# Second part of a two-level Winograd kernel in a written order, its buffers over those of the first part, bias through ScalarE

## The chip, the cores and the metric

The kernel runs on one core of one Trainium2 chip. The metric is the device time of one execution in microseconds. The engines named below are TensorE (PE; its weight loads are a row of their own, PEld), VectorE (DVE), ScalarE (ACT), GpSimd (POOL) and SyncE (SP), which here only issues transfers. Each engine works through its own queue in order and waits on semaphores for the others.

## The reference

Everything is fp32. There are 8 batches of 256 tokens with 1024 features, and 8 adapter matrices of 1024 x 1024, one of which is chosen for each batch by an index.

```python
w = weight[adapter_ids]                       # (8, 1024, 1024)
y = einsum('bsi,boi->bso', x, w)
base_out = einsum('btd,od->bto', y, base_W) + base_b
logits = einsum('btd,nd->btn', y, router_W) + router_b      # 15 columns
topk_p, topk_i = top_k(softmax(logits), 8)
w = einsum('btk,btke->bte', topk_p, onehot(expert_map[topk_i]))
h = einsum('btd,erd->bter', y, A)             # 8 experts of rank 16
lora = einsum('bter,eor->bto', h * w[..., None], B) * 2.0
out = x + base_out + lora
```

## The kernel before, in words

**First part (lines 161 to 431).** For each batch b it computes y = W x with one level of Winograd's scheme: seven block products instead of eight, each of 16 matmuls (128x128 by 128x128), accumulated in three PSUM tiles pa, pb, pc. VectorE makes the sums of weight blocks (`first_sum`, `other_sums`) and of x blocks (`turns`), and adds PSUM results into y. The weight tiles `wt` (8 buffers of 8 KB a partition) come by transfers. Two further things are threaded through this loop, each one batch behind. `project` multiplies y of batch b-1 by the router's and the LoRA's down matrices, ScalarE copies h and takes Exp; `weigh` (VectorE) makes softmax, the eight largest, and hw = h times its weights; `turn` transposes hw on TensorE and ScalarE copies it to `hwTs`. `prepare(n)` makes, on VectorE, a share of the 14 sums and raw blocks of base_W that the second part's left sides need, and stores them to two DRAM tiles, left_raw and left_sum (n = 0 to 3 writes entries 0 to 2, n = 4 to 7 entries 3 to 6). This whole part stands under `manual_schedule` for TensorE, VectorE, ScalarE and SP: their instructions run in the order in which the program writes them. After the loop come the turn of batch 6, the projection of batch 7, and `weigh` and `turn` of batch 7 (lines 428 to 431).

**Second part (lines 435 to 607).** base_W y is done with two levels of the same scheme, for two groups of four batches. A group has seven outer products, called with left numbers 0, 1, 3, 5, 4, 6, 2; each (`product`, line 470) has again seven inner blocks of 4 matmuls (128x128 by 128x256), in the order a11, s1, s2, a12, s3, s4, a22. Four of the seven carry LoRA terms: 8 more matmuls by hwT and up (line 461), two each in blocks s1, a12, s4 and a22. A product loads its two left tiles, makes four differences t1 to t4 of its right side on VectorE (line 487, tiles `lt`), and drains PSUM seven times: four times with `take` (a copy by ScalarE, line 504, where there is no base to add; an add by VectorE, lines 497 and 500, where there is) and three times with `add`. Blocks a11, s2, s3 and a22 accumulate one after the other in the same PSUM tile pa, so each of the last three may begin only when the drain of the one before has read pa. In the last product of all, pa is split in two tiles, pa and pe.

The right sides are y's blocks and running differences of them: b11, t2, b12 and b21 are remade on VectorE with whole-block subtractions of 2048 elements a partition (lines 584, 586, 593, 598). Four of the products give results; `residual` loads the tile xt of x and adds it and the bias (line 557, two scalar_tensor_tensors of 128x256), and `store` writes the result out.

The second part is not under `manual_schedule`. The framework's planner orders its instructions, and it may mix them with the end of the first part. Buffers are placed pool by pool: when the pools of the first part close, those of the second take their place in memory from the start, and a tile may be written only when all tiles that lay there before have been read for the last time. Here the first pool of the second part is t2, then the `lt` tiles, then u and v, the result tiles q and the tiles xt.

Of the kernel before, what the change touches and what calls it, by code (L numbers as in the profile page):

```python
# [27 lines left out]
def kernel(  # L28
# [21 lines left out]
    KH = 4  # L50
# [12 lines left out]
    wpool = ctx.enter_context(tc.tile_pool(name="w", bufs=8))  # L63
    dram = ctx.enter_context(
# [11 lines left out]
    em_i = const.tile([P, N], I32, name="em_i")  # L76
    bb = const.tile([P, KC], F32, name="bb")

# [37 lines left out]
    def weigh(h, ex, route, rpool):  # L116
# [28 lines left out]
        hw = rpool.tile([P, NTT, ER], F32, name="hw")  # L145
# [7 lines left out]
    def turn(b, hw, ident, ps_t):  # L153

        pt = ps_t.tile([P, S], F32, name="pt")
        for j in range(NTT):
            nc.tensor.transpose(pt[:, ts(j, P)], hw[:, j, :], ident)  # L157
        nc.scalar.copy(hwTs[b // GB][:, b % GB // 2, b % 2, :], pt)


    with ExitStack() as phase:
        cpool = phase.enter_context(tc.tile_pool(name="c1", bufs=1))
        xpool = phase.enter_context(tc.tile_pool(name="x", bufs=2))
        tpool = phase.enter_context(tc.tile_pool(name="t", bufs=2))
        rpool = phase.enter_context(tc.tile_pool(name="route", bufs=2))
        mpool = phase.enter_context(tc.tile_pool(name="m", bufs=1))
# [7 lines left out]
        ps_t = phase.enter_context(  # L174
            tc.tile_pool(name="ps_t", bufs=1, space=bass.MemoryType.PSUM)
        )

        ident = cpool.tile([P, P], F32, name="ident")
        make_identity(nc, ident)
# [5 lines left out]
        def constants():  # L185
            nc.sync.dma_start(rb, router_b.to_broadcast([P, N]))
            nc.sync.dma_start(em_i, emap.to_broadcast([P, N]))
            nc.sync.dma_start(bb, base_b)
            nc.sync.dma_start(ar_sb.rearrange("p k n -> p (k n)"), ar)
            nc.vector.tensor_copy(em_f, em_i)  # L190
            for e in range(E):
                nc.vector.tensor_scalar(
                    route[:, e, :], em_f, float(e), SCALING, ALU.is_equal, ALU.mult
                )
# [113 lines left out]
        def turns(x):  # L308

            b11, b12, b21, b22 = x[:, 0, 0], x[:, 0, 1], x[:, 1, 0], x[:, 1, 1]  # L310
            t1 = tpool.tile([P, KH, P], F32, name="t1")
            nc.vector.tensor_sub(t1, b12, b11)
            t2 = tpool.tile([P, KH, P], F32, name="t2")
            nc.vector.tensor_sub(t2, b22, t1)
            t4 = tpool.tile([P, KH, P], F32, name="t4")
            nc.vector.tensor_sub(t4, b21, t2)
            nc.vector.tensor_sub(b12, b22, b12)
            return t1, t2, t4
# [21 lines left out]
        EN = mybir.EngineType  # L340
# [13 lines left out]
        for b in range(B):  # L354
# [22 lines left out]
            if waiting:  # L377
                turn(*waiting, ident, ps_t)
# [28 lines left out]
            else:  # L407
                block(pa, q["a21"], b12, False)
                nc.vector.tensor_add(out(1, 1), pa, m5)
                hw = weigh(h, ex, route, rpool)  # L410
                waiting = b - 1, hw
                block(pc, q["s4"], b22, False)
                if last:
                    nc.vector.tensor_add(out(0, 1), pc, u2)
                    prepare(b)
                block(pa, q["a22"], t4, False)
                nc.scalar.copy(out(1, 0), pa)
# [10 lines left out]
        turn(*waiting, ident, ps_t)  # L428

        h, ex = project(B - 1, ar_sb, rpool, ps_h, (1, 0))  # L430
        turn(B - 1, weigh(h, ex, route, rpool), ident, ps_t)
# [3 lines left out]
    with ExitStack() as phase:  # L435
        tpool = phase.enter_context(tc.tile_pool(name="t2", bufs=1))
        lpool = phase.enter_context(tc.tile_pool(name="l2", bufs=8))
        mpool = phase.enter_context(tc.tile_pool(name="m2", bufs=1))
        qpool = phase.enter_context(tc.tile_pool(name="q2", bufs=6))
        xpool = phase.enter_context(tc.tile_pool(name="x2", bufs=3))  # L440
# [5 lines left out]
        )  # L446

# [22 lines left out]
        def product(left, right, base, into, u=None, hw=None, split=False):  # L470


            ra = wpool.tile([P, NS, 4 * P], F32, name="wt")
            nc.sync.dma_start(
                ra.rearrange("p s f -> p (s f)"), left_raw[left].rearrange("p s f -> p (s f)")
            )
            su = wpool.tile([P, NS, 3 * P], F32, name="wt")
            nc.sync.dma_start(
                su.rearrange("p s f -> p (s f)"), left_sum[left].rearrange("p s f -> p (s f)")
            )  # L480
            a11, a12, s3, a22 = (ra[:, :, ts(n, P)] for n in range(4))
            s1, s2, s4 = (su[:, :, ts(n, P)] for n in range(3))
            b11, b12, b21, b22 = right[:, 0, 0], right[:, 0, 1], right[:, 1, 0], right[:, 1, 1]

            def minus(x, y):
                t = lpool.tile([P, 2, S], F32, name="lt")
                nc.vector.tensor_sub(t, x, y)  # L487
                return t

            t1 = minus(b12, b11)  # L490
            t2 = minus(b22, t1)
            t3 = minus(b22, b12)
            t4 = minus(b21, t2)

            def add(dst, acc, other):
                if acc[0] is acc[1]:
                    nc.vector.tensor_add(dst, acc[0], other)  # L497
                else:
                    for mi in range(2):
                        nc.vector.tensor_add(dst[:, mi], acc[mi][:, mi], other[:, mi])  # L500

            def take(dst, acc, i, j):
                if base is None:
                    nc.scalar.copy(dst, acc[0])
                else:
                    add(dst, acc, base(i, j))
# [7 lines left out]

            pa = 2 * [ps.tile([P, 2, S], F32, name="pa")]
# [5 lines left out]
            c11, c12, c21, c22 = into(0, 0), into(0, 1), into(1, 0), into(1, 1)  # L521
            block(pa, a11, b11, True)
            take(c11, pa, 0, 0)
            block(pc, s1, t1, True, *term(1, 1))
            take(c22, pc, 1, 1)
            block(pa, s2, t2, False)
            take(c12, pa, 0, 1)
            block(pb, a12, b21, True, *term(0, 0))
            add(c11, pb, c11)
            yield 0, 0, c11  # L530
            block(pa, s3, t3, False)
            add(c22, pa, c22)
            yield 1, 1, c22
            block(pc, s4, b22, False, *term(0, 1))
            add(c12, pc, c12)
            yield 0, 1, c12
            block(pa, a22, t4, False, *term(1, 0))
            take(c21, pa, 1, 0)
            yield 1, 0, c21
# [3 lines left out]

        for g in range(B // GB):
            y, hw = ys[g], hwTs[g]

# [3 lines left out]
            def residual(oh, th, i, j, q):  # L550

                n = number(oh, th, i, j)
                xt = xpool.tile([P, 2, S], F32, name="xt")
                nc.sync.dma_start(xt.rearrange("p m t -> p (m t)"), xr[n])
                for mi in range(2):
                    c = oh * KH + 2 * i + mi
                    nc.vector.scalar_tensor_tensor(  # L557
                        q[:, mi], xt[:, mi], bb[:, c : c + 1], q[:, mi], ALU.add, ALU.add
                    )

            def store(oh, th, i, j, q):
                n = number(oh, th, i, j)
                nc.sync.dma_start(outq[n], q.rearrange("p m t -> p (m t)"))

            def finish(*r):
                residual(*r)
                store(*r)

            def flat(t):
                return t.rearrange("p i j k o -> p (i j k o)")  # L570

            b11, b12, b21, b22 = y[:, 0, 0], y[:, 0, 1], y[:, 1, 0], y[:, 1, 1]
            u = mpool.tile([P, 2, 2, 2, S], F32, name="u")
            v = mpool.tile([P, 2, 2, 2, S], F32, name="v")
# [3 lines left out]


            for _ in product(0, b11, None, at(u)):  # L580
                pass
            for r in product(1, b21, at(u), fresh, 0, hw[:, 0]):
                finish(0, 0, *r)
            nc.vector.tensor_sub(flat(b11), flat(b12), flat(b11))
            t2 = tpool.tile([P, 2, 2, 2, S], F32, name="t2")
            nc.vector.tensor_sub(flat(t2), flat(b22), flat(b11))
            for _ in product(3, t2, at(u), at(u)):
                pass
            for _ in product(5, b11, at(u), at(v), 1, hw[:, 1]):
                pass  # L590
            for r in product(4, b22, at(v), fresh, 2, hw[:, 1]):
                finish(0, 1, *r)
            nc.vector.tensor_sub(flat(b12), flat(b22), flat(b12))
            for i, j, q in product(6, b12, None, fresh):
                nc.vector.tensor_add(u[:, i, j], u[:, i, j], q)
                nc.vector.tensor_add(q, v[:, i, j], q)
                finish(1, 1, i, j, q)
            nc.vector.tensor_sub(flat(b21), flat(b21), flat(t2))
            end = g == B // GB - 1
            if end:  # L600
                residual(1, 0, 1, 0, u[:, 1, 0])
            for i, j, q in product(2, b21, at(u), fresh, 1, hw[:, 0], end):
                if end and (i, j) == (1, 0):
                    for mi in range(2):
                        nc.sync.dma_start(outq[number(1, 0, 1, 0), :, ts(mi, S)], q[:, mi])
                else:
                    finish(1, 0, i, j, q)
# [69 lines left out]
```

## Time and profile before

| | |
|---|---|
| median of 3 runs | 445.47 us (445.07 to 446.3) |
| profiled execution | 445.35 us |
| its span | 443.6 us |
| granted TensorE clock | 0.999 |
| TensorE busy | 436.4 us (98%) |
| VectorE busy | 306.4 us (69%) |
| ScalarE busy | 36.3 us (8%) |
| first block of the second part starts | 241.51 us |
| last matmul record starts | 439.71 us or just after (two records, 0.59 us together) |

The span runs from the first to the last instruction of the profiled execution; the device time has 1.77 us around it. An fp32 matmul leaves two records on TensorE and two on the row of its weight loads. In a timeline a line has the start, the length (of all merged instructions), the engine, the program's line, the operation, the tiles, the count, and in square brackets the idle time before it and who ended it. Matmul records overlap by about 0.16 us, so the distance from start to start says more than a length.

### The profile page before, as it was taken

The page shows a single profiled execution, that of the slowest core. Times are in us where ns is not written, and L with a number is a line of the kernel's source. Part 1 is how long each engine was busy: PE and PEld are TensorE (multiplying, and loading weights), DVE is VectorE, ACT ScalarE, POOL GpSimd, SP SyncE. Part 2 cuts the span into 40 slices and gives each one's busy share as a digit, 9 for nine tenths or more (in the row PEclk, how much of TensorE's full clock was granted, in tenths as well). Part 3 has the DMA queues.
Part 4 walks back from the last instruction along what each step waited for, and adds up shares of the span by engine and source line. Part 5 has one row for each costly group of instructions (what it writes and reads, how often), then busy time and mean ns, then how long its engine had stood idle before and what let it go on. Part 6 is the DMA issues. An engine that isn't in the chain of part 4 may idle for free.

```text
span 443.6 us, 7251 instructions
## 1 busy us (share of the span) xinstructions
PE 436.4 (98%) x2996; PEld 410.2 (92%) x2996; DVE 306.4 (69%) x523; ACT 36.3 (8%) x73; POOL 0.7 (0%) x6
## 2 busy tenths in 40 slices
PE   6999999999999999999999999999999999999997
PEld 6999999999999999999999788888888888888885
DVE  0579597582973967949629599746598399546494
ACT  1110101011011110110111100000100100000100
POOL 0000000000000000000000000000000000000000
PEclk9999999999999999999999999999999999999999
DMA  7998978678597687894872968622969738601463
GB/s 235 399 396 305 327 268 310 225 284 291 190 287 258 250 273 277 287 329 140 271 295 103 389 243 280 242 97 100 310 228 276 277 112 287 236 0 53 139 183 125
DMA packets 35122, 106.19 MB, mean 239 GB/s; under 512 B 3090, under 2 KB 6930, under 8 KB 31890
## 3 DMA queue, kind: packets, MB, share of 16 engines
q1 hardware_dynamic: 35090, 105.74, 68.7%
q8 instruction: 23, 0.38, 0.3%
q14 instruction: 9, 0.07, 0.1%
HBM read 84.49 MB, written 21.23 MB: 238 GB/s over the span
## 4 chain that ended last, share of the span: by engine, by line
PE 93%; DVE 4%; DMA 1%; SPq 1%; issue 0%
PE pa L214 24%; PE pa L452 21%; PE pc L214 12%; PE pc L452 11%; PE pb L214 7%; PE ph L97 6%; PE pb L452 5%; PE pc L461 3%; PE pb L461 2%; PE pa L461 1%; DMA wt<-in_w_dram 1%; DVE lt L487 1%; PE pe L452 1%; PE pt L157 0%; DVE w L144 0%
## 5 line engine op out<-in xcount | busy, mean ns | idle before, releaser
L452 PE MATMUL pa<-lt,wt 128*128 128x256 f32 x324 | 78.4, 380 | 0.0
L452 PEld LDWEIGHTS pa<-lt,wt 128*128 128x128 f32 x324 | 61.1, 190 | 9.5 <-DVE u L497 0.6
L214 PE MATMUL pa<-x,wt 128*128 128x128 f32 x512 | 59.9, 275 | 2.1 <-DMA wt<-in_w_dram 2.1
L214 PEld LDWEIGHTS pa<-x,wt 128*128 128x128 f32 x512 | 58.5, 192 | 2.5 <-issue 1.3
L214 PE MATMUL pa<-t,wt 128*128 128x128 f32 x480 | 56.1, 275 | 0.0
L214 PEld LDWEIGHTS pa<-t,wt 128*128 128x128 f32 x480 | 54.8, 192 | 0.0
L106 DVE TENSOR_TENSOR lg<-ph,rb 128x30 f32<-128x30 f32 x8 | 1.5, 189 | 47.3 <-ACT h L105 47.3
L97 PE MATMUL ph<-ar_sb,y 128*128 128x143 f32 x256 | 32.7, 285 | 0.0
L97 PEld LDWEIGHTS ph<-ar_sb,y 128*128 128x128 f32 x256 | 31.9, 190 | 0.0
L214 PE MATMUL pb<-x,wt 128*128 128x128 f32 x256 | 30.0, 275 | 0.0
L214 PE MATMUL pc<-t,wt 128*128 128x128 f32 x256 | 29.9, 275 | 0.0
L214 PE MATMUL pc<-x,wt 128*128 128x128 f32 x256 | 29.9, 275 | 0.0
L214 PEld LDWEIGHTS pb<-x,wt 128*128 128x128 f32 x256 | 29.2, 192 | 0.0
L214 PEld LDWEIGHTS pc<-t,wt 128*128 128x128 f32 x256 | 29.2, 192 | 0.0
L214 PEld LDWEIGHTS pc<-x,wt 128*128 128x128 f32 x256 | 29.2, 192 | 0.0
L452 PE MATMUL pc<-lt,wt 128*128 128x256 f32 x112 | 27.9, 379 | 0.0
L557 DVE SCALAR_TENSOR_TENSOR q<-xt,bb,q 128x256 f32<-128x256 f32 x62 | 27.0, 478 | 0.4
L452 PE MATMUL pc<-y,wt 128*128 128x256 f32 x96 | 24.1, 379 | 0.0
L452 PE MATMUL pb<-y,wt 128*128 128x256 f32 x96 | 24.1, 379 | 0.0
L452 PEld LDWEIGHTS pc<-lt,wt 128*128 128x128 f32 x112 | 21.3, 190 | 2.9
L325 DVE TENSOR_TENSOR wt<-wt 128x2048 f32<-128x2048 f32 (+1 forms) x9 | 18.5, 2051 | 6.5 <-DMA wt<-in_wq_dram 6.5
L452 PE MATMUL pa<-y,wt 128*128 128x256 f32 x92 | 22.1, 379 | 0.0
(117 smaller groups left out, 482.7 us busy)
## 6 DMA issues: line engine op xcount, KB each, us to landing
wt<-in_wq_dram SPq DMA_DIRECT2D x21, 1024.0 KB, 6.3
wt<-left_raw SPq DMA_DIRECT2D x14, 1024.0 KB, 5.7
wt<-left_sum SPq DMA_DIRECT2D x14, 768.0 KB, 6.5
xt<-in_xr_dram SPq DMA_DIRECT2D x32, 256.0 KB, 3.4
out_dram<-q SPq DMA_DIRECT2D x31, 256.0 KB, 2.5
x<-in_xq_dram SPq DMA_DIRECT2D x7, 1024.0 KB, 6.3
wt<-in_w_dram SPq DMA_DIRECT2D x7, 1024.0 KB, 5.4
spare<-in_bq_dram SPq DMA_DIRECT2D x4, 1024.0 KB, 5.5
```

Of the source, the lines that this page charges most:

```text
L97: nc.tensor.matmul(ph[:, j], lhsT=y[:, k // KH, th, k % KH // 2, bi, k % 2, ts(j, P)], rhs=ar_sb[:, k, :], start=(j == order[0] and k == 0 ...
L106: nc.vector.tensor_add(lg, ph[:, :, ER:], rb.unsqueeze(1).to_broadcast([P, NTT, N]))
L214: mm = nc.tensor.matmul(acc[:, m // 2, m % 2, :], lhsT=left[:, k, ts(m, P)], rhs=right[:, k, :], start=(first and n == 0), stop=(k == KH - 1),
L325: nc.vector.tensor_add(q["s1"][:, h], q["a21"][:, h], q["a22"][:, h])
L452: nc.tensor.matmul(acc[mi][:, mi, :], lhsT=left[:, 2 * k + mi, :], rhs=right[:, k, :], start=(first and k == 0 and (mi == 0 or acc[0] is n ...
L461: nc.tensor.matmul(acc[mi][:, mi, :], lhsT=up[:, ts(mi, P)], rhs=hw, start=False, stop=True, skip_group_check=True,)
L487: nc.vector.tensor_sub(t, x, y)
L557: nc.vector.scalar_tensor_tensor(q[:, mi], xt[:, mi], bb[:, c : c + 1], q[:, mi], ALU.add, ALU.add)
```

## The change

The second part is put under `manual_schedule` too, and its order is written out.

- Each of the seven products has seven gaps, one ahead of each block. In a gap the program first appends steps to two queues, `soon` and `later`, and then runs up to two of them (`fill(2)`), `soon` first. The steps are VectorE instructions: the differences of the next product (two in gap 0, one each in gaps 3 and 4), the subtractions that remake b11, t2, b12 and b21, now in quarters of 512 elements a partition, the joint additions of product 5, and the residual additions with the stores behind them. The drains of the blocks stand in the program between the gaps.
- The left tiles are loaded by `load_left`: those of products 0 and 1 near the end of the first part, those of product n + 2 in gap 5 of product n. The tiles of x are loaded in gaps 0 to 3 of the product that needs them (6 buffers instead of 3).
- The four differences of the first product are made in the last turn of the first loop, ahead of `prepare(7)`. In the first part and the second the difference tiles share one pool, `tt`, of 6 buffers.
- The turn of batch 7 moves from the end of the first part to behind the first product of the second. Its hw lies in a pool of its own; the identity and the transposes' PSUM tile now live through both parts.
- The pools are opened in another order: in the first part x, m, c1, then the routing pool and prep; in the second m2 (u and t2), q2, x2, v. So u and t2 lie over x, q over m and c1, the tiles of x over the routing pool and prep.
- The bias is added by ScalarE: in products 0 and 5 of a group each `take` becomes two activations (Identity, 128x256) with the bias as a pointer operand. Product 5 uses the difference of the two halves of the bias, made once by a VectorE subtraction in `constants`. The residual is then one VectorE add of 128x512.

The matmuls are the same in number and form. The diff, cut to its core:

```diff
@@ weigh, load_left, differences
-    def weigh(h, ex, route, rpool):
+    def weigh(h, ex, route, rpool, hwpool):
...
-        hw = rpool.tile([P, NTT, ER], F32, name="hw")
+        hw = hwpool.tile([P, NTT, ER], F32, name="hw")
...
+    def differences(right):
...
+                t[n] = tpool.tile([P, 2 * S], F32, name="tt").rearrange(
+                    "p (k o) -> p k o", k=2
+                )
+                x, y = (t[v] if isinstance(v, int) else v for v in (of, less))
+                nc.vector.tensor_sub(t[n], x, y)
...
+        return [minus(1, b12, b11), minus(2, b22, 1), minus(3, b22, b12), minus(4, b21, 2)]
...
@@ constants
+            nc.vector.tensor_sub(bb[:, KH:], bb[:, KH:], bb[:, :KH])
...
@@ last turn of the first loop, and its end
                 if last:
                     nc.vector.tensor_add(out(0, 1), pc, u2)
+                    left[0] = load_left(lefts[0])
+                    terms = [step() for step in differences(ys[0][:, 0, 0])]
                     prepare(b)
                 block(pa, q["a22"], t4, False)
+                if last:
+                    left[1] = load_left(lefts[1])
                 nc.scalar.copy(out(1, 0), pa)
...
-        turn(*waiting, ident, ps_t)
-
-        h, ex = project(B - 1, ar_sb, rpool, ps_h, (1, 0))
-        turn(B - 1, weigh(h, ex, route, rpool), ident, ps_t)
+
+        turn(*waiting)
+        nh, nex = project(B - 1, ar_sb, rpool, ps_h, (1, 0))
+        waiting = B - 1, weigh(nh, nex, route, rpool, const)
...
@@ second part
+        soon, later = deque(), deque()
+
+        def fill(n):
+            for _ in range(n):
+                if soon or later:
+                    soon.popleft()() if soon else later.popleft()[1]()
...
             def take(dst, acc, i, j):
-                if base is None:
-                    nc.scalar.copy(dst, acc[0])
+                if isinstance(base, int):
+                    for mi in range(2):
+                        c = base + 2 * i + mi
+                        nc.scalar.activation(
+                            dst[:, mi], acc[mi][:, mi], AF.Identity, bias=bb[:, c : c + 1]
+                        )
                 else:
-                    add(dst, acc, base(i, j))
+                    plus(dst, acc, base(i, j))
...
+            def gap(n):
+                for step in gaps.get(n, ()):
+                    step()
+                fill(2)
...
+            gap(0)
             block(pa, a11, b11, True)
-            take(c11, pa, 0, 0)
+            take(c[0, 0], pa, 0, 0)
+            gap(1)
             block(pc, s1, t1, True, *term(1, 1))
-            take(c22, pc, 1, 1)
+            take(c[1, 1], pc, 1, 1)
+            gap(2)
             block(pa, s2, t2, False)
-            take(c12, pa, 0, 1)
+            take(c[0, 1], pa, 0, 1)
+            gap(3)
             block(pb, a12, b21, True, *term(0, 0))
-            add(c11, pb, c11)
-            yield 0, 0, c11
+            plus(c[0, 0], pb, c[0, 0])
+            done(0, 0, c[0, 0])
+            gap(4)
             block(pa, s3, t3, False)
-            add(c22, pa, c22)
-            yield 1, 1, c22
+            plus(c[1, 1], pa, c[1, 1])
+            done(1, 1, c[1, 1])
+            gap(5)
             block(pc, s4, b22, False, *term(0, 1))
-            add(c12, pc, c12)
-            yield 0, 1, c12
+            plus(c[0, 1], pc, c[0, 1])
+            done(0, 1, c[0, 1])
+            gap(6)
             block(pa, a22, t4, False, *term(1, 0))
...
+            fill(len(soon))
+            while later and later[0][0] not in (c[0, 1], c[1, 0]):
+                later.popleft()[1]()
+            done(1, 0, c[1, 0])
...
-                for mi in range(2):
-                    c = oh * KH + 2 * i + mi
-                    nc.vector.scalar_tensor_tensor(
-                        q[:, mi], xt[:, mi], bb[:, c : c + 1], q[:, mi], ALU.add, ALU.add
-                    )
...
+                    def run():
+                        add(q, q, x)
+                        nc.sync.dma_start(outq[n], q.rearrange("p m t -> p (m t)"))
+
+                    later.append((q, run))
...
+                for q in quarters:
+                    soon.extend(update(b11, b12, b11, [q]))
+                    soon.extend(update(t2, b22, b11, [q]))
...
+                steps = [steps[:2], steps[2:3], steps[3:]]
+                for k, m in ((0, 0), (3, 1), (4, 2)):
+                    gaps[k].append(advance(m, steps))
+                if n == 0:
+                    gaps[1].append(lambda: first_terms((0, 0), (0, 1)))
+                    gaps[4].append(lambda: first_terms((1, 0)))
+                    gaps[6].append(lambda: first_terms((1, 1)))
+                elif n in outer:
+                    gaps[1].append(lambda n=n: soon.extend(outer[n]))
+                if n in result_of:
+                    for k, ij in enumerate([(0, 0), (1, 1), (0, 1), (1, 0)]):
+                        gaps[k].append(lambda r=result_of[n] + ij: load_x(*r))
...
+                if here + 2 < len(lefts):
+
+                    def fetch(m=here + 2):
+                        left[m] = load_left(lefts[m])
+
+                    gaps[5].append(fetch)
+                product(
+                    left.pop(here), terms, right, base, into, done, gaps, *up_hw,
+                    *([None] * (2 - len(up_hw))), end and n == 6
+                )
+                terms = nexts
+                if here == 0:
+                    turn(*waiting)
```

## The prediction

> **What bounds the kernel now.** I read the page's first part, then busy time by stage, then TensorE's and VectorE's timelines around the hand-over between the two parts, since the change alters only that hand-over and what follows it.
>
> The page's head and two stages (length; then per engine the busy time and instruction count, in the order PE, PEld, DVE, ACT, POOL):
>
> ```profile
> PE 436.4 (98%) x2996; PEld 410.2 (92%) x2996; DVE 306.4 (69%) x523; ACT 36.3 (8%) x73; POOL 0.7 (0%) x6
> ...
> 241.51:253.60 12.09, 11.57 (x56) 9.77 (x55) 7.69 (x26) 2.54 (x6) 0.00 (x0) 1.00 1.03 383
> 241.51:440.15 198.64, 198.12 (x916) 172.62 (x914) 142.91 (x245) 10.16 (x19) 0.00 (x0) 1.00 0.58 202
> ```
>
> The second part runs from 241.51 to 440.15. TensorE is busy there for all but 0.52 us, at full clock. VectorE is busy 143 of 199 us: not the bound, but not idle either. TensorE's timeline where the parts meet:
>
> ```profile
> 237.59 4.09 PE L97 MATMUL ph<-ar_sb,y 128*128 128x143 f32 x32
> 241.51 1.89 PE L452 MATMUL pa<-y,wt 128*128 128x256 f32 x8
> 243.24 1.89 PE L452 MATMUL pc<-lt,wt 128*128 128x256 f32 x8
> 244.97 1.89 PE L452 MATMUL pb<-y,wt 128*128 128x256 f32 x8
> 246.69 1.03 PE L452 MATMUL pa<-y,wt 128*128 128x256 f32 x4
> 248.24 0.41 PE L157 MATMUL pt<-ident,hw 128*128 128x128 f32 x2 [0.52 <-DVE hw L146]
> ```
>
> A block of four matmuls (eight records) takes 1.727 us from start to start, so one matmul takes 0.432 us. Second part: 14 products x 28 matmuls + 64 LoRA matmuls = 456, or 196.9 us, and the last transposes 0.24: 241.51 + 197.14 = 438.65. It really ends at 440.14 (last two records start at 439.71, 0.43 long). So **1.49 us is all that TensorE loses in the second part**: 0.69 at 248.24 (4 records from 246.69 should end at 247.55), 0.33 just after it, 0.29 in the split last product, the rest in single blips of about 0.1.
>
> VectorE at the same place:
>
> ```profile
> 242.32 0.68 DVE L487 TENSOR_TENSOR lt<-y 128x512 f32<-128x512 f32 x1
> 242.93 0.18 DVE L106 TENSOR_TENSOR lg<-ph,rb 128x30 f32<-128x30 f32 x1
> ...
> 247.67 0.42 DVE L146 TENSOR_TENSOR hw<-h,w 128x256 f32<-128x256 f32 x1
> 249.57 0.69 DVE L497 TENSOR_TENSOR u<-pb,u 128x512 f32<-128x512 f32 x1 [1.49 <-ACT u L504]
> 250.35 0.69 DVE L497 TENSOR_TENSOR q<-pa,u 128x512 f32<-128x512 f32 x1
> 254.45 0.69 DVE L497 TENSOR_TENSOR u<-pa,u 128x512 f32<-128x512 f32 x1 [3.40 <-PE pa L452]
> 255.24 0.69 DVE L497 TENSOR_TENSOR u<-pc,u 128x512 f32<-128x512 f32 x1
> 255.85 2.28 DVE L584 TENSOR_TENSOR y<-y 128x2048 f32<-128x2048 f32 x1
> 258.23 2.29 DVE L586 TENSOR_TENSOR t<-y 128x2048 f32<-128x2048 f32 x1
> ```
>
> VectorE is solidly busy until hw of the last batch (248.09). Then it idles 1.49 and 3.40 us, and makes the operands b11 and t2 of the third product only at 255.85 (L584, L586). A 128x512 add holds VectorE 0.605 us when independent of the one before (242.32 to 242.93), about 0.72 when it reads that one's result.
>
> [...] The trace has no such form; its nearest rows are a 128x256 copy of 0.37 and a 128x512 copy of 0.59. [...] one table load of 1.28 us in the whole run, although Exp and copies alternate.
>
> **The change part by part.**
>
> *The last turn goes behind product 0.* TensorE no longer waits for hw: minus 0.69. Its followers (0.33) go too: in the old order ScalarE's copy of the turned hw (248.68) stood ahead of product 0's first drains, and the buffer u lay where it could be written only then. Now u lies over the first part's x, last read by the block ending at 237.4. The turned weights are needed first in group 1, about 100 us later.
>
> *Bias by ScalarE.* 62+2 scalar_tensor_tensors of 0.476, issued in pairs of about 0.79, become 32 adds of 0.605: 25 to 19 us of VectorE. In products 0 and 5 each drain becomes two activations: [...] (0.74 by the copies) against 0.59. Each has the whole next block (1.73) before TensorE needs that bank, so it costs nothing[...]. First case: exp ends near 243.47, [...] the bank is wanted at 244.97. One extra tiny subtraction on bb sits at 43.3, its data asked for at 27.1: nothing.
>
> *Transfers.* On SP the first left pair is queued ahead of the last prepare's two stores, so it has landed by about 232. The second pair stands behind these stores: 1.0 + 0.75 MB out and as much in, from about 243.1 at the 380 GB/s that the stages of 241 to 245 show, is 9.2 us: landed near 252.5 to 253.5, against a need of 253.8. Later pairs are issued two products ahead, residual tiles at least 3 us ahead.
>
> *The fixed VectorE order at the hand-over: this is where it costs.* The old order ran the differences of products 0 and 1 (8 adds) before hw. Now only product 0's four come before, and product 1's plus the quarters of b11 and t2 are strewn, two per gap, **ahead** of product 0's own additions. Step by step:
>
> 1. The add at L414 starts at 234.00, as now. Four differences, two bubbles of 0.115: prepare starts at 237.14. Its eight adds, spaced as now (four of 0.72 and so on), bring the router's first add to 242.57.
> 2. lg, mx, sub: 0.63. Exp on ScalarE: 243.24 to 243.47. den starts at 243.65. From den to the end of hw takes 3.04 (231.03 to 234.07 a batch earlier): hw ends at 246.69. Four fewer adds make this 1.4 earlier than now.
> 3. Next, in written order: t1, t2 (gap 0), b11 and t2 quarter 00 (gap 1), b11 and t2 quarter 01 (gap 2), t3 (gap 3), the addition of pb to c[0,0], t4 and b11 quarter 10 (gap 4), and **the addition of pa to c[1,1]**. The ten starts ahead of this last one: 7 x 0.605 + 3 x 0.72 = 6.4. It runs 253.1 to 253.8.
> 4. TensorE's last block of product 0 accumulates into that same pa. Unhindered it would start at 241.51 + 24 x 0.432 = 251.87. It must wait for the read: 253.8 + 0.05 (as 429.00 to 429.06 in the split tail). **Stall: 1.95 us.** Behind it in TensorE's queue stand the turn and all of product 1.
>
> After that VectorE catches up. I walked the whole second part with these spacings, 0.20 from a block's end to the add that reads it, two filled steps per gap. A plain product gives VectorE 15 adds (about 9.8 us) per 12.1 us of TensorE, a LoRA one 15 per 15.5. The tight one is product 5: 19 adds, 12.4 us against 12.1. Its backlog of five runs into product 6, whose first drain then ends 0.24 us before TensorE wants the bank. No other stall. In the split last product each half is read a block ahead of need, so its 0.29 goes as well.
>
> Sum: -1.34 (the 1.49 less 0.15 of blips that I leave in) + 1.95 = +0.6 us on the profiled execution's 445.35 (span 443.58 and 1.77 around it): 445.95. The tail after TensorE (3.4 us) is the same two half stores. The runs' median is 445.47, 0.12 above the profiled one. I take **446.0**.
>
> **Rivals.**
>
> *A. Small loss or none (above).* For it: each step has a row. Likeliest own range: 445.2 to 446.8, from an hw that ends 0.8 earlier or later; each us moves the stall by a us.
>
> *B. The stall isn't there.* If VectorE gets its steps done 1.95 us earlier, what is left is -1.34: 444.1. For it: 1.95 is only three adds. Against it: hw would have to end by 244.7, before the router's chain allows. This is also the most there is to win, 0.3% of the run, as nothing else of TensorE's is touched.
>
> *C. Slower: VectorE as late as now.* If hw ends at 248.1 as in the kernel before, the stall is 3.36 and the time 445.35 - 1.34 + 3.36 = 447.4. It decides from hw at about 247.5. For it: the router's chain shares VectorE with prepare in strict order and has an Exp on another engine in its middle. The same mechanism at its worst: if every filled step pays 0.72 rather than 0.605[...] the walk gives 2.9 at this place and 2.2 more in products 2, 6 and 9: about 449. Against it: independent adds run at 0.605 in this trace wherever they stand together.
>
> *D. The change doesn't do what it says*, in that the buffers still hold something back: u, t2 over x, and q over m1, u2 and ar_sb have all been released by 241.5; the residual tiles over the prepare buffer, by the stores' landing near 250. It would need over 3 us of lateness to be seen. I put it into C's chance.
>
> **How the numbers follow.** About 0.3% is what a measurement of this kernel can tell from no change: 444.1 to 446.8. A 0.70, B 0.10, C with D 0.20. A lies nearly all inside the 0.3%; a few hundredths fall over its upper edge and about as many of C fall under it. So faster 0.10, same 0.69, slower 0.21. The range takes in B's end, all of A and C's first bound, not its worst: 444.0 to 447.4.
>
> **What would show it.** Right: TensorE idle once, about 2 us before product 0's last block (near 251.9), released by the VectorE addition of pa to c[1,1]; hw ending near 246.7; no wait of the transposes for hw; product 1 starting near 255.8; [...] VectorE's residual adds at 0.68; TensorE's last matmul ending near 440.7. Wrong: that block starting at 251.9 (B), hw after 247.5, or waits of TensorE in products 2, 5, 6 (C), a TensorE wait on a left tile (D).

## The result and the profile after

The changed kernel takes 443.85 us (median of 7 runs, 443.4 to 444.2) against 445.47 us before: a ratio of 0.9965, with a 95% interval of 0.9951 to 0.998. A second series gave 443.84 us and 0.9965 (0.9952 to 0.9978). So it is 0.35% faster, where a loss of 0.5 us was forecast (446.0, range 444.0 to 447.4), and 0.15 us under the lower edge of that range. The prediction's rival B named 444.1.

Stages of the changed kernel (length; then per engine the busy time and count, in the order PE, PEld, DVE, ACT, POOL; then clock, transfer share and GB/s). The first row is as long as product 0's 28 matmuls take at TensorE's own pace, the second the whole second part:

```profile
240.69:252.78 12.09, 11.99 (x57) 10.24 (x56) 11.85 (x34) 3.01 (x8) 0.00 (x0) 1.00 0.81 288
240.69:438.20 197.51, 197.41 (x916) 173.01 (x914) 139.56 (x237) 14.19 (x35) 0.00 (x0) 1.00 0.59 213
```

From the first block to the last matmul it is 197.51 us where it was 198.63. The prediction's sum without any gap is 197.14; the one kernel below that runs without a gap takes 197.06, so that TensorE really lost 1.57 us before, not 1.49. **Of these, 1.12 us are gone.** VectorE is now busy 11.85 of the 12.09 us of product 0. It was busy 7.69 us of the same length before: it had waited, and now it doesn't.

The rest of the difference between the two profiled executions lies ahead of the second part, which starts at 240.69 instead of 241.51. That is chance: in a second profile of each kernel the starts were 241.79 (after) and 241.29 (before), while the stretches came out as 197.48 and 198.66. The start hangs on the first 40 us, in which the first weights land: TensorE's waits for them in these four profiles add up to 1.5 to 2.8 us. From the 300th matmul record (39 to 40 us in) to the second part's first block all four take 201.74 or 201.75 us. I therefore compare the kernels by this stretch, which repeats within 0.03 us, beside their ratios. The medians differ by 1.6 us, some 0.4 to 0.5 more than the stretch explains; with an interval of 0.6 us to either side of the ratio I don't look for a cause of that.

TensorE's timeline where the parts meet:

```profile
249.32 1.89 PE L507 MATMUL pc<-y,wt 128*128 128x256 f32 x8
251.31 1.99 PE L507 MATMUL pa<-tt,wt 128*128 128x256 f32 x8
253.14 0.38 PE L202 MATMUL pt<-ident,hw 128*128 128x128 f32 x2
253.36 1.89 PE L507 MATMUL pa<-y,wt 128*128 128x256 f32 x8
255.09 1.10 PE L507 MATMUL pc<-tt,wt 128*128 128x256 f32 x4
256.03 0.59 PE L516 MATMUL pc<-hwT,up 128*128 128x256 f32 x2
```

The last block of product 0 starts 1.99 us after the block before it, where 1.727 is the pace. The stall that I had put at 1.95 us is there, in the very place, but it is 0.26. The block itself then takes 1.83 us to the transposes, 0.10 more than the pace; the block behind the wait in one_order (253.46 to 255.29) and in before_turn (248.56 to 250.39) takes 1.83 too. With 0.07 more in product 1 that makes up what is left, 0.44. The transposes wait for nothing. VectorE's timeline shows why the stall is short:

```profile
236.91 0.69 DVE L185 TENSOR_TENSOR tt<-y 128x512 f32<-128x512 f32 x1
...
238.11 0.69 DVE L185 TENSOR_TENSOR tt<-y,tt 128x512 f32<-128x512 f32 x1
...
242.71 0.18 DVE L115 TENSOR_TENSOR lg<-ph,rb 128x30 f32<-128x30 f32 x1
242.81 0.68 DVE L659 TENSOR_TENSOR y<-y 128x512 f32<-128x512 f32 x1
243.40 0.18 DVE L119 TENSOR_REDUCE mx<-lg 128x2 f32<-128x30 f32 x1
243.52 0.69 DVE L659 TENSOR_TENSOR t<-y 128x512 f32<-128x512 f32 x1
244.13 0.18 DVE L120 TENSOR_TENSOR lg<-lg,mx 128x30 f32<-128x30 f32 x1
244.23 0.68 DVE L659 TENSOR_TENSOR y<-y 128x512 f32<-128x512 f32 x1
244.84 0.18 DVE L128 TENSOR_REDUCE den<-ex 128x2 f32<-128x30 f32 x1
244.95 0.69 DVE L659 TENSOR_TENSOR t<-y 128x512 f32<-128x512 f32 x1
...
245.64 0.67 DVE L185 TENSOR_TENSOR tt<-y 128x512 f32<-128x512 f32 x1
...
248.43 0.43 DVE L155 TENSOR_TENSOR hw<-h,w 128x256 f32<-128x256 f32 x1
248.77 0.68 DVE L537 TENSOR_TENSOR u<-pb,u 128x512 f32<-128x512 f32 x1
249.37 0.68 DVE L185 TENSOR_TENSOR tt<-y,tt 128x512 f32<-128x512 f32 x1
249.97 0.68 DVE L659 TENSOR_TENSOR y<-y 128x512 f32<-128x512 f32 x1
250.57 0.68 DVE L537 TENSOR_TENSOR u<-pa,u 128x512 f32<-128x512 f32 x1
```

Steps of the second part (L659 and L185 are its subtractions) stand between the links of the router's last chain (L115 to L155), which belongs to the first part. Each part keeps its own written order, but **the two orders are merged**. Of the ten instructions that I had put between hw and the addition of pa to c[1,1], the first seven (the L185 and L659 lines above hw) run before hw. So hw ends 8.17 us after the second part's start instead of the 5.18 that I had worked out, but nobody waits for it any more; the addition of pa to c[1,1] ends at 251.25, and TensorE follows at 251.31.

### The profile page after: what moved, and what is told of

Read it like the earlier page. It is cut to its first block, busy times and chain, and to the rows that moved or that the text cites. A ratio compares the mean times of both kernels' runs of the same rounds, so it can differ in the third digit from the quotient of the medians.

```text
span 441.6 us, 7255 instructions
## 1 busy us (share of the span) xinstructions
PE 435.1 (99%) x2996; PEld 410.1 (93%) x2996; DVE 303.1 (69%) x516; ACT 40.4 (9%) x89; POOL 0.7 (0%) x6
## 4 chain that ended last, share of the span: by engine, by line
PE 92%; DVE 5%; DMA 1%; SPq 1%; issue 1%
PE pa L253 24%; PE pa L507 20%; PE pc L253 12%; PE pc L507 10%; PE pb L253 7%; PE ph L106 6%; PE pb L507 5%; PE pc L516 3%; PE pb L516 2%; PE pa L516 1%; DMA wt<-in_w_dram 1%; DVE tt L185 1%; PE pe L507 1%; DVE y L659 0%; PE pt L202 0%
## 5 line engine op out<-in xcount | busy, mean ns | idle before, releaser
L507 PE MATMUL pa<-tt,wt 128*128 128x256 f32 x324 | 78.0, 379 | 0.1
L507 PEld LDWEIGHTS pa<-tt,wt 128*128 128x128 f32 x324 | 61.4, 190 | 8.9 <-DVE u L537 0.5
L253 PE MATMUL pa<-tt,wt 128*128 128x128 f32 x480 | 56.1, 275 | 0.0
L253 PEld LDWEIGHTS pa<-tt,wt 128*128 128x128 f32 x480 | 54.8, 192 | 0.0
L115 DVE TENSOR_TENSOR lg<-ph,rb 128x30 f32<-128x30 f32 x8 | 1.5, 189 | 48.6 <-ACT h L114 48.6
L253 PE MATMUL pc<-tt,wt 128*128 128x128 f32 x256 | 29.9, 275 | 0.0
L253 PEld LDWEIGHTS pc<-tt,wt 128*128 128x128 f32 x256 | 29.2, 192 | 0.0
L507 PE MATMUL pc<-tt,wt 128*128 128x256 f32 x112 | 27.8, 380 | 0.0
L507 PEld LDWEIGHTS pc<-tt,wt 128*128 128x128 f32 x112 | 21.2, 190 | 3.0 <-DMA wt<-left_sum 0.2
L630 DVE TENSOR_TENSOR q<-q,xt 128x512 f32<-128x512 f32 x31 | 21.3, 688 | 0.5
```

The costliest lines, as they stand in the source:

```text
L115: nc.vector.tensor_add(lg, ph[:, :, ER:], rb.unsqueeze(1).to_broadcast([P, NTT, N]))
L253: mm = nc.tensor.matmul(acc[:, m // 2, m % 2, :], lhsT=left[:, k, ts(m, P)], rhs=right[:, k, :], start=(first and n == 0), stop=(k == KH - 1),
L507: nc.tensor.matmul(acc[mi][:, mi, :], lhsT=left[:, 2 * k + mi, :], rhs=right[:, k, :], start=(first and k == 0 and (mi == 0 or acc[0] is n ...
L630: add(q, q, x)
```

## The experiments

The stretch is that from the second part's first block to the last matmul; the shortest, 197.06, has no gap. Each stretch comes from one profile. In the diffs, dots stand for lines left out.

| kernel | ratio to before | stretch us | TensorE's largest wait in product 0 |
|---|---|---|---|
| before, second profile | 0.9997 (0.9985 to 1.0009) | 198.66 | 0.68, for hw |
| changed, second profile | 0.9965 (0.9952 to 0.9978) | 197.48 | 0.26, for VectorE |
| one_order | 1.0008 (0.9999 to 1.0018) | 198.96 | 1.78, for VectorE |
| before_turn | 1.0017 (1.0006 to 1.0027) | 199.01 | 0.85, for ScalarE |
| before_turn_pools | 0.9979 (0.997 to 0.9988) | 197.98 | none |
| u_late | 1.0157 (1.0135 to 1.0179) | 205.95 | 6.36, for ScalarE |
| bias_vector | 0.9985 (0.9973 to 0.9996) | 198.02 | 0.26, for VectorE |
| turn_early | 0.9999 (0.9987 to 1.0011) | 198.48 | 1.38, for hw |
| fill_one | 0.9982 (0.9965 to 0.9999) | 197.56 | none |
| left_first | 0.9971 (0.9961 to 0.9982) | 197.42 | 0.25, for VectorE |
| left_first_fill_one | 0.996 (0.9947 to 0.9973) | 197.06 | none |

**Repeats.** Both kernels unchanged, for the scatter.

> The changed kernel as it is. Theory M (the two written orders are merged, so VectorE does part of the second part's steps in the router's pauses): a ratio to the kernel before near 0.9965, the stall ahead of product 0's last block 0.2 to 0.4 us again, TensorE's stretch from the second part's first block to its last matmul 197.5 us. The start of that stretch, 240.7 in the first profile, is expected anywhere from 240.6 to 241.6, since it hangs on the first weights' arrival; if it comes out near 240.7 every time, the first part has gained something too.

> The kernel before as it is, for the scatter. Ratio 1.000 within 0.001. Its second part begins at 241.51 in the first profile; if the start is chance it comes out anywhere from 240.6 to 241.6 here, and if the first part differs between the kernels, near 241.5 again. TensorE's second stretch 198.6 us with the wait for hw of about 0.5 to 0.7 us.

As told above: the stretches and the waits repeat, and the starts scatter, that of the changed kernel a little beyond the range expected (241.79). A gain in the first part is not there: from the 300th matmul record to the second part all the kernels of the table take 201.73 to 201.75 us, and what comes before scatters by 3 us.

**Is it the merging?** Both parts under one written order:

```diff
-        phase.enter_context(
+        ctx.enter_context(
             tc.manual_schedule(engines={EN.PE, EN.DVE, EN.Activation, EN.SP})
         )
...
-        phase.enter_context(
-            tc.manual_schedule(engines={EN.PE, EN.DVE, EN.Activation, EN.SP})
-        )
```

> Both parts under one written order instead of two; nothing else. Theory M: VectorE then runs all of product 0's steps behind the router's last chain, as the prediction assumed; hw ends near 246 (0.8 less if the second part starts 0.8 earlier), TensorE stalls 1.9 us ahead of product 0's last block, and the kernel takes 1.7 us more than the changed one: ratio to before 1.000. Rival S (the prediction's walk is wrong in its spacings, the order is not what matters): no more than the 0.26 us stall of the changed kernel, ratio 0.9965.

VectorE's timeline of this kernel, and from the table of waits the line in which TensorE waits for it (waiter, line, whom for: us, times, longest):

```profile
242.37 0.18 DVE L115 TENSOR_TENSOR lg<-ph,rb 128x30 f32<-128x30 f32 x1
242.59 0.18 DVE L119 TENSOR_REDUCE mx<-lg 128x2 f32<-128x30 f32 x1
...
243.35 0.18 DVE L128 TENSOR_REDUCE den<-ex 128x2 f32<-128x30 f32 x1 [0.35 <-ACT ex L122]
...
245.99 0.42 DVE L155 TENSOR_TENSOR hw<-h,w 128x256 f32<-128x256 f32 x1
246.33 0.68 DVE L185 TENSOR_TENSOR tt<-y 128x512 f32<-128x512 f32 x1
247.05 0.69 DVE L185 TENSOR_TENSOR tt<-y,tt 128x512 f32<-128x512 f32 x1
247.66 0.68 DVE L656 TENSOR_TENSOR y<-y 128x512 f32<-128x512 f32 x1
...
250.92 0.68 DVE L534 TENSOR_TENSOR u<-pb,u 128x512 f32<-128x512 f32 x1
251.52 0.68 DVE L185 TENSOR_TENSOR tt<-y,tt 128x512 f32<-128x512 f32 x1
252.12 0.68 DVE L656 TENSOR_TENSOR y<-y 128x512 f32<-128x512 f32 x1
252.72 0.68 DVE L534 TENSOR_TENSOR u<-pa,u 128x512 f32<-128x512 f32 x1
```

```profile
PE pa L504 <- DVE u L534: 1.6, 1, 1.6
```

This is the order that the prediction walked. hw ends 5.1 us after the second part's start (predicted 5.2), the addition of pa to c[1,1] ends 12.1 after it (12.3), the stall is 1.78 (1.95), and the median 445.58 us. The expectation M is met, S falls. The two kernels run the same VectorE instructions in number and kind (516). From the start of the last addition of the first part's loop (L452) to that of the addition of pa to c[1,1] it is 233.80 to 252.72, or 18.92 us, in one order and 233.18 to 250.57, or 17.39, when merged. The 1.53 between them are pauses that the other order fills. About 0.9 lie in the router's chain from lg to pr: a link of it takes 0.20 to 0.22 us alone (as 242.37 to 242.59 here) and 0.08 to 0.12 beside an independent add (as 242.71 to 242.81 when merged), and VectorE idles 0.35 here for Exp. About 0.25 lie between `prepare`'s additions, where two differences now stand, and about 0.35 between steps of the second part that read one another's results. The stall differs by 1.52.

**The turn alone.** The kernel before, with the last turn held behind product 0 on TensorE by an added dependency, its hw and the identity in the lasting pool `const` (which is also where the changed kernel has them):

```diff
-        turn(B - 1, weigh(h, ex, route, rpool), ident, ps_t)
+        waiting = B - 1, weigh(h, ex, route, rpool, const)
...
             for _ in product(0, b11, None, at(u)):
                 pass
+            if g == 0:
+                turn(*waiting, ident, ps_t)
```

> The kernel before with one part of the change: the turn of the last batch stands behind product 0 on TensorE (its hw and the identity in the lasting pool). Theory: the 0.69 us wait at hw goes, and the 0.33 us of followers with it if they come from ScalarE's copy standing ahead of product 0's drains: TensorE's second stretch 197.6 to 198.0 instead of 198.6, ratio 0.998 to 0.9985. Rival: the wait only takes another form, since u still lies where the routing tiles lay and can be written only when hw is done: ratio 1.000, with TensorE waiting for a drain in product 0 instead.

The rival holds: the wait only changes its form, and the stretch is 0.4 us longer than before. ScalarE's timeline of this kernel:

```profile
244.33 0.23 ACT L118 ACTIVATE ex<-lg 128x30 f32<-128x30 f32 x1 [2.48 <-DVE lg L116]
247.92 0.58 ACT L516 COPY u<-pa 128x512 f32<-128x512 f32 x1 [3.36 <-DVE hw L151]
```

The block a11 was ready at 242.95, but u lies where routing tiles lay, so its copy waits for hw itself. TensorE then waits 0.85 us for that copy. In the kernel before, the wait for hw covers most of this second one.

**The turn and the placement.** On top of before_turn the pools are opened so that u and v lie over x; order by the planner and bias by VectorE remain.

```diff
-        cpool = phase.enter_context(tc.tile_pool(name="c1", bufs=1))
         xpool = phase.enter_context(tc.tile_pool(name="x", bufs=2))
         tpool = phase.enter_context(tc.tile_pool(name="t", bufs=2))
+        mpool = phase.enter_context(tc.tile_pool(name="m", bufs=1))
+        cpool = phase.enter_context(tc.tile_pool(name="c1", bufs=1))
         rpool = phase.enter_context(tc.tile_pool(name="route", bufs=2))
-        mpool = phase.enter_context(tc.tile_pool(name="m", bufs=1))
...
-        tpool = phase.enter_context(tc.tile_pool(name="t2", bufs=1))
+        mpool = phase.enter_context(tc.tile_pool(name="m2", bufs=1))
         lpool = phase.enter_context(tc.tile_pool(name="l2", bufs=8))
-        mpool = phase.enter_context(tc.tile_pool(name="m2", bufs=1))
+        tpool = phase.enter_context(tc.tile_pool(name="t2", bufs=1))
```

> The kernel before with two parts of the change: the last turn behind product 0, and the pools opened in such an order that u and v lie over the first part's x; the second part is still ordered by the planner, bias still by VectorE. Theory P (turn and placement together are the gain, the written order and the bias add nothing): TensorE's second stretch 197.4 to 197.7 instead of 198.6, no wait in product 0, ratio 0.9965 to 0.998. Rival W (the written order is what brings the gain): stretch 198.4 or more, ratio 0.999 to 1.001.

Both gaps of product 0 are gone, but the stretch is 197.98, not 197.4 to 197.7: it lies between P and W, though the ratio is within P's. Of the 1.12 to 1.18 us gained in all, the turn and the placement together bring 0.65. The 0.92 still above the shortest stretch are gaps of 0.03 to 0.10 each, by the distance from start to start: 0.33 in the split last product and 0.13 at 356, which the kernel before has too, and 0.45 in product 2, where it has 0.06. The written order has none of these.

**The placement alone, reversed.** The changed kernel with v and q ahead of u and t2, which then lie over m, c1, the routing pool and prep.

```diff
-        mpool = phase.enter_context(tc.tile_pool(name="m2", bufs=1))
+        vpool = phase.enter_context(tc.tile_pool(name="v", bufs=1))
         qpool = phase.enter_context(tc.tile_pool(name="q2", bufs=6))
+        mpool = phase.enter_context(tc.tile_pool(name="m2", bufs=1))
         xpool = phase.enter_context(tc.tile_pool(name="x2", bufs=6))
-        vpool = phase.enter_context(tc.tile_pool(name="v", bufs=1))
```

> The changed kernel with the second part's pools in another order: v and q first, so that u and t2 lie over the end of m, over c1 and over the routing pool, which are read until hw of the last batch is made. Theory P: ScalarE's drains of product 0 wait for that, near 248 to 249, and since TensorE's order is fixed it stands: a stall of 3 to 6 us ahead of s2 or s3, ratio 1.003 to 1.010. Rival W (placement is of no account, only the order): ratio 0.9965.

Worse than expected. TensorE waits 6.36 us ahead of s2. The line of ScalarE's timeline that ends this wait:

```profile
252.51 0.84 ACT L546 ACTIVATE u<-pa,bb 128x256 f32<-128x256 f32 x2 [5.49 <-DMA left_sum<-spare]
```

ScalarE's first drain waits not for the routing chain (hw ends at 250.10) but for the last prepare's store out of its buffer, which also lay underneath. Busy time by stage (columns as above) shows what came on top:

```profile
246.00:253.40 7.40, 1.20 (x7) 0.72 (x5) 4.40 (x20) 1.12 (x4) 0.00 (x0) 0.83 1.02 342
253.40:257.00 3.60, 3.60 (x9) 2.88 (x10) 1.63 (x3) 0.67 (x2) 0.00 (x0) 0.50 1.01 423
```

After the wait the granted clock is 0.50, and one block takes 3.57 us (253.40 to 256.97) instead of 1.73.

**The turn in the changed kernel.** Put back inside product 0:

```diff
-                if here == 0:
-                    turn(*waiting)
...
+                if here == 0:
+                    gaps[4].append(lambda: turn(*waiting))
```

> The changed kernel with the last turn inside product 0, between its blocks a12 and s3, about where the kernel before has it. Theory: TensorE then waits there until hw is made, 7.9 to 8.2 us after the second part's start against 6.9 at which it arrives: a wait of 1.2 to 1.4 us, in which VectorE gets far enough for the 0.26 us ahead of the last block to vanish. Second stretch 198.4 to 198.6, ratio 0.9985 to 0.9995, so that moving the turn is worth about as much as the whole change. Rival: the turn's place matters little with u lying over x: stretch 197.5, ratio 0.9965.

A wait of 1.38 us for hw, stretch 198.48, both as expected, and nearly the whole gain is gone: the stretch is 0.15 us under that of the kernel before, and the ratio (0.9999) can't be told from 1. With the merged order hw comes later than it did before, so in this kernel the turn has to stand behind product 0.

**The bias.** Back to VectorE: one copy by ScalarE for a drain, two scalar_tensor_tensors for a residual.

```diff
-                        nc.scalar.activation(
-                            dst[:, mi], acc[mi][:, mi], AF.Identity, bias=bb[:, c : c + 1]
-                        )
+                    nc.scalar.copy(dst, acc[0])
...
-                        add(q, q, x)
+                            nc.vector.scalar_tensor_tensor(
+                                q[:, mi], x[:, mi], bb[:, c : c + 1], q[:, mi], ALU.add, ALU.add
+                            )
```

> The changed kernel with the bias added by VectorE as before: one ScalarE copy for a drain, pairs of scalar_tensor_tensors for a residual. The prediction's claim that the bias part costs and brings nothing: the same as the changed kernel within noise, ratio 0.996 to 0.9975; VectorE about 6 us busier in all, product 5's backlog larger, at most 0.3 us of a stall in product 6. Rival: the fixed order leaves VectorE so little room that this relief is needed: stalls in products 2, 5 and 6 of both groups, ratio 0.998 or more.

The stretch is 198.02, 0.5 us more than with the bias on ScalarE: gaps of 0.21 in product 1 and 0.39 in product 6 of the first group, against 0.07 and none. Those in product 1 lie about the start of its second block (255.97), the place where the weight loads of the changed kernel wait 0.21 us for left_sum, so the 0.13 more need not come from the bias. TensorE's timeline at product 6:

```profile
329.02 0.59 PE L515 MATMUL pc<-hwT,up 128*128 128x256 f32 x2
329.74 1.56 PE L506 MATMUL pa<-tt,wt 128*128 128x256 f32 x6
```

Two records take 0.43, not 0.72: the backlog of product 5 reaches the first drain of product 6, an addition by VectorE that here ends at 329.68. VectorE is busy 145.5 us in the second part, against 139.6. Neither expectation fits wholly: the wait of 0.29 is within the 0.3 that the theory allowed, but the ratio is the rival's, whose other stalls are missing. The kernel is also the written order with the turn and the placement but without the bias on ScalarE, and its 198.02 are no less than the 197.98 that turn and placement reach under the planner: in these profiles the written order gains only together with the relief of VectorE. Neither the order nor the bias was tried alone on the kernel before. The intervals of the two ratios just overlap (0.9973 to 0.9996 against 0.9952 to 0.9978), so it is the stretch that tells them apart, from one profile of this kernel.

**What is left.** One step fewer in gap 4 of product 0:

```diff
-                fill(2)
+                fill(1 if early and n == 4 else 2)
```

> The changed kernel with one step instead of two filled in gap 4 of product 0, so that the addition of pa to c[1,1] comes one step earlier. Theory M: it ends 0.6 us sooner, the 0.26 us stall is gone, TensorE's second stretch 197.2 to 197.3 and the ratio 0.996, hardly to be told from the changed kernel by time. Rival: something else released that block: the stall stays at 0.26.

The stall goes as expected, which shows what released that block, but the stretch doesn't fall. TensorE's weight loads now wait for both left tiles of product 1, 0.3 us each (in the changed kernel for left_sum alone, 0.2):

```profile
PEld pa L507 <- DMA wt<-left_raw: 0.3, 1, 0.3
PEld pc L507 <- DMA wt<-left_sum: 0.3, 1, 0.3
```

Product 1 now comes early enough to meet its own left tiles. So these were moved up on SP:

```diff
                 if last:
                     nc.vector.tensor_add(out(0, 1), pc, u2)
                     left[0] = load_left(lefts[0])
                     terms = [step() for step in differences(ys[0][:, 0, 0])]
-                    prepare(b)
                 block(pa, q["a22"], t4, False)
                 if last:
                     left[1] = load_left(lefts[1])
+                    prepare(b)
```

> The changed kernel with the second pair of left tiles queued on SP ahead of the last prepare's two stores instead of behind them. Theory: these tiles then land before product 1 in any case, and the small delays of product 1 (0.08 us in the changed kernel) go; the 0.26 us ahead of product 0's last block stays. Stretch 197.3 to 197.5, not to be told from the changed kernel by time.

> Both: second left pair ahead of the stores, and one step instead of two filled in gap 4 of product 0. Theory: with the drain a step earlier and the tiles there in time, product 0's end and product 1 run without a gap: stretch 197.15 to 197.3, 0.25 us under the changed kernel, ratio to before 0.9958 to 0.9965. Rival: something else holds product 1 back, as it did when only the step was taken out (stretch 197.56).

The first comes out as expected; the second does better than the 197.15 that it put lowest. Together they leave no gap in the second part: of 197.06 us TensorE is busy for 197.06, and no record starts late. The stage (columns as above):

```profile
240.58:437.64 197.06, 197.06 (x916) 173.18 (x914) 139.47 (x237) 14.16 (x35) 0.00 (x0) 1.00 0.57 204
```

Its median is 443.58 us. It beats the kernel before for certain (0.996, 0.9947 to 0.9973); over the changed kernel it has 0.45 us in the stretch, which the ratios of the two can't tell apart.

## Why the prediction was wrong, step by step

- *What bounds the kernel; the 1.49 us to win.* Right, but for 0.08 us: left_first_fill_one wins all there is, 1.57. Nothing was won elsewhere.
- *The turn behind product 0, minus 0.69, and its followers, minus 0.33.* The wait is gone and both amounts were won, but not by the turn alone: before_turn loses as much at ScalarE. The prediction named the reason (u can be written only when the routing tiles are done), yet counted it as a side effect; it is the other half of the same gain. Turn and placement together bring 0.65 of the 1.12; the rest came with the written order (no gaps in product 2, at 356 and in the last product) and the bias together, less the 0.37 of the new stall and 0.07 in product 1.
- *The bias costs nothing.* Two activations take 0.84 us (one has 0.471), where two of the copies that the profile of before shows would be 0.74; what an activation with a bias takes was not shown there. They are hidden: the first pair ends at 243.50, and TensorE comes back to that tile at 244.14. What I missed is that the 6 us taken off VectorE are worth 0.4 us: with the slower residuals the backlog of product 5, 0.24 us from doing harm in my walk, does it.
- *The second left pair lands at 252.5 to 253.5.* Nearly: in the changed kernel 123 of the 128 packets of left_sum had ended by 253.4. The last five ended one after another, 0.23 us apart, until 254.55, and the weight loads of product 1 waited 0.2 us, until 255.06. Why these five are late stays open. The prediction's sign of rival D, a TensorE wait on a left tile, thus came, but it cost only 0.07 us, because the block before it was late too: in fill_one, where that block is on time, product 1 loses 0.49 us.
- ***The fixed VectorE order at the hand-over*: step 3 is what failed.** I took the second part's steps to come after the first part's last chain, because they are written after it. There are two written orders, one for each part, and the trace shows them merged: seven of the ten instructions that I put between hw and the addition of pa to c[1,1] run before hw. So the stall that step 4 puts at 1.95 us was 0.26. The durations, the chain of waits and the place of the stall were right: in one_order, where the order is as I assumed, each of them comes out within 0.2 us, and the time (445.58) within 0.1% of the forecast. The profile of before had two hints. The second part's differences (L487) stood between lg, mx and sub there; I read that as the planner's doing and took it to end where both sides are written out. And step 2 takes four additions out ahead of hw, 4 x 0.605 = 2.4 us, yet has hw only 1.4 earlier: the 1.0 between them are pauses that the differences had filled. (Step 1 names two bubbles of 0.115; its sum has one, and so has the trace of one_order.)
- *Rival B.* It was this case, priced at 444.1, and dismissed because hw could not end by 244.7. It didn't: it ended later still, after the 247.5 that I had named as the sign of rival C, and the steps simply did not wait for it. I had tied two things together that only my order tied. That B's number is near the measured one is luck in so far as its condition never came.
- *Rival C and the upper half of the range* rested on the same order. The lower end, 444.0, was the profiled execution's sum without a stall (445.35 - 1.34), with no allowance for the runs' scatter of 0.4 us to either side.

## What to carry to other kernels

When a hand-written order ends and another begins, ask whether the second is ordered against the first or only within itself: here that alone is worth 1.5 us, since dependent instructions, above all a chain of small ones, left pauses which independent work of the next stage filled (0.20 to 0.22 us from link to link of the router's chain in one_order, 0.08 to 0.12 where an add stands between). When a wait is moved away, look at what lay covered by it: here a buffer that comes free at the same moment made TensorE wait 0.85 us in before_turn, where it had waited 0.69, and the two had to be removed together. In a kernel whose bound engine is 98% busy, count the gaps first, since they are the most that a reordering can win.

## What the runs showed of the hardware

After TensorE had idled for 6.20 us in u_late (247.20 to 253.40) it ran at a granted clock of 0.50 (stage 253.40 to 257.00), and a block of 1.73 us took 3.57. The mean clock is 1.00 in the stage 240 to 246, 0.83 from 246.00 to 253.40, and 0.92 from 257.00 to 262.00. An estimate from these means, which takes the clock to have been either 1.00 or 0.50, puts the half clock from about 250.9, some 3.7 us after TensorE had stopped, to about 257.8. The 1.78 us in one_order left the clock at 1.00 (stage 241 to 257). The stall in u_late thus cost more than its length: of the 8.9 us that its stretch lies above the shortest, 6.36 are the wait, 1.84 the first block at half clock, 0.40 the block behind it (256.97 to 259.10), and 0.29 a gap near 340.
